# ScalarE's order in the first step of an attention unit: exponential, denominators' copy, logit copies, exponential

## The chip, the core and the metric

The kernel runs on one core of a Trainium2 chip. The metric is the device time of one execution in microseconds (us), the median over several runs. A profiled execution, taken apart from those, gives the span from its first to its last instruction and a record of every instruction.

Five engines work side by side, each through its own instruction stream: TensorE (PE in the profile, with its weight loads as PEld), VectorE (DVE), ScalarE (ACT), GpSimd (POOL) and SyncE (SP), which here only issues DMA transfers.

## What is computed

The input is 8 images of 512 channels and 32 x 32 positions, all in 32-bit floats. The work is two residual layers, each ahead of a group norm:

```
x = x + L0(groupnorm(x))
x = x + L1(groupnorm(x))

L0:  t = silu(bn(conv1x1(x)))                  512 -> 512, split in two halves of 256
     ys = [t[:256], t[256:]]
     for i in 0, 1:
         z = silu(bn(conv3x3(ys[-1])))         256 -> 256
         q, k, v = conv1x1(z)                  4 heads of 64
         logits = q . (k + r) / 8              1024 x 1024 a head, r = rw + rh
         z = softmax(logits) . v
         ys.append(ys[-1] + silu(bn(conv1x1(z))))
     out = silu(bn(conv1x1(concat(ys))))       1024 -> 512

L1:  a 1x1 convolution whose weights are masked by the arg-max of two tables and permuted
```

The softmax is the part that the change is about. For a query i it needs the maximum of its logits over the 1024 keys, the exponentials of the logits less that maximum, their sum (the denominator), and the product of the exponentials with v, divided by the denominator.

## The kernel before

**Slots and units.** An image has two attention blocks, and a *slot* is one block of one image; there are 16 slots, and the images go through them in pairs. A slot is cut into four *units*: two pairs of heads (`hp`) by two halves of 512 queries (`half`). So there are 64 units. A unit handles two heads at once, one in each half of a tile's second axis, with queries along the free axis and 128 keys at a time on the partitions: eight key tiles, `t` from 0 to 7. The exponentials of a key tile stand in an `st` tile of 128 x 2 x 512.

**What a unit does**, by the methods of class `Unit`:

- `logits(t)` (line 503): two matmuls into two PSUM banks `lg`; ScalarE copies both to `st` (line 518); VectorE keeps the running maximum `mx` (line 523).
- `top()` and `spread()` (lines 525 and 534): transposes on TensorE and a reduction on VectorE (line 532) turn `mx` into the negated maximum of each query, and transposes spread it over the partitions in the PSUM tile `mb`.
- `soften(t)` (line 543): VectorE adds `mb` to `st` in place (line 545).
- `exponent(t)` (line 547): ScalarE takes the exponential of `st` in place (line 549); GpSimd adds it into the sum `acc` in four pieces (line 556), from t = 1 on.
- `values(t)` (line 558): two matmuls of v with `st` accumulate into the PSUM tile `po` over all t (line 563).
- `finish()` (line 572): matmuls of `acc` with ones give the denominators in a PSUM bank `den` (line 577); ScalarE copies them to the tile `rb` (line 580).
- `divide(part)` (line 582): VectorE takes the reciprocal of half of `rb` (line 584) and multiplies `po` with it into `q` (line 586).

**The pipeline over units.** The main loop goes through the units. A unit's logits are made one unit ahead, while the unit before it is in its exponentials. The inner loop (line 1057) has four steps, t = 0, 2, 4 and 6, each for two key tiles. In the first step, t = 0, the unit before (`before`) is brought to its end: its denominators, its last two value products, its division. Beside that the step softens the unit's own tiles 0 and 1, takes their exponentials, and makes logits 0 and 1 of the next unit (`nxt`). In a step t > 0 the order is: soften t and t + 1, exponential of t, value products of t - 2 and t - 1, logits t and t + 1 of the next unit, exponential of t + 1.

**Background work.** Between these steps `advance` emits pieces of other work: the 1x1 and 3x3 convolutions of other images, their batch norms with Silu on ScalarE (`bn_silu`, line 130), group norms (line 165), the projections to q, k and v, and the last layer. The 3x3 convolution is computed from transformed rows: VectorE makes its inputs (lines 280 to 288).

**What sets the order.** The compiler orders each engine's instructions itself, by program order and by when it thinks that they can run, except where the kernel forbids it. Three helpers do so: `pe_turn`, `in_turn` and `act_turn` tie an instruction to the one before that went through the same helper, on TensorE, VectorE and ScalarE. On ScalarE the logit copies and the exponentials are in this chain; the batch norms, the group norms and, before the change, the denominators' copy are not. The two reciprocals and the two products of `divide` are not in VectorE's chain either. Waits between engines are added by the compiler.

**Buffers.** PSUM is cut into three pools: `ps_m` with the one `mb` tile (two banks' worth), `ps_o` with one buffer for `po`, and `ps_f` with five banks that `lg`, `den`, the transposed maxima and all convolutions share. There are ten `st` tiles. The tile `rb` comes from a pool of three that the background's batch norms share.

The core of the order in a step:

```
                u.soften(t)
                u.soften(t + 1)
                if t:
                    u.exponent(t)
                ...
                    lag.values((t - 2) % KT)
                    lag.values((t - 1) % KT)
                ...
                    nxt.logits(t)
                    nxt.logits(t + 1)
                ...
                if not t:
                    u.exponent(t)
                u.exponent(t + 1)
```

Of the kernel before, what the change touches and what calls it, by code (L numbers as in the profile page):

```python
# [39 lines left out]
def conv_preact_kernel(ctx: ExitStack, tc: tile.TileContext, x, cv1, cv2, mcv1, qkv, mcv2, bn, rw, rh, conv, s_in, t_in, out):  # L40
    nc = tc.nc
# [26 lines left out]
    def bank(name):  # L68
        return ps_f.tile([P, HALF], F32, tag="bank", name=name)

    def half_tile(name):
        return tp.tile([P, HALF], F32, tag="t", name=name)
# [115 lines left out]
    def act_turn(instruction):  # L188

        if act_last:  # L190
            tc.add_manual_dep(instruction.ins, act_last.pop().ins.name, IN_ORDER, reason="order of ScalarE")
        act_last.append(instruction)
# [3 lines left out]
    def pe_turn(instruction):  # L196

        if pe_last:
            tc.add_manual_dep(instruction.ins, pe_last.pop().ins.name, IN_ORDER, reason="order of TensorE")
        pe_last.append(instruction)  # L200
# [293 lines left out]
    class Unit:  # L494
# [76 lines left out]

        def finish(self):

            den = bank(f"den_{self.name}")
            for h in range(2):
                pe_turn(
                    nc.tensor.matmul(den[HD * h : HD * h + HD], ones[:, :HD], self.acc[:, h], start=True, stop=True)  # L577
                )
            self.rb = half_tile(f"rb_{self.name}")
            nc.scalar.copy(self.rb, den)  # L580

        def divide(self, part):
            r = ts(part, HALF // 2)
# [325 lines left out]
    def slot_filler(s):  # L909

        prev = slots[s - 1] if s else (None, 0)
        nxt = slots[s + 1] if s + 1 < len(slots) else (None, 0)
        todo, needed = [], 0.0

        def add(us, g):
            nonlocal needed
            todo.append((us, g))
            needed += us

        im, i = nxt  # L920
        add(8.0, bg.take(8.0))
        if im and i == 1:
            add(7.0, im.conv_m2(0))
            add(0.0, call(im.transform, 1, 3.0, 1.0))
            add(9.0, bg.take(9.0))
        products = im.conv3(i) if im else iter(())
        if prev[1] == 1:
            if im:
                add(21.3, (us for _, us in zip(range(16), products)))
            add(7.0, prev[0].conv_m2(1))  # L930
            add(0.0, call(lambda: finishing(prev[0])))
        if im:
            add(10.7 if prev[1] == 1 else 32.0, products)
            add(7.0, bg.take(7.0))
        if im:
            add(21.0, im.project(i))
        if s + 2 < len(slots) and slots[s + 2][1] == 0:
            add(0.0, call(slots[s + 2][0].load_y))
            add(0.0, call(slots[s + 2][0].transform, 0, 8.0, 1.3))
        rest = SHARE - needed if im else 70.0  # L940
        if rest > 0:
            todo.append((rest, bg.take(rest, wait=True)))
        total = sum(c for c, _ in todo)
        return needed, total, todo
# [76 lines left out]
    before = None  # L1021
    for s in range(len(slots)):
        needed, total, todo = slot_filler(s)
        state = {"done": 0.0}

        def filler():
            for us, g in todo:
                start = state["done"]
                for cost in g:
                    clock.tick(cost)  # L1030
                    state["done"] += cost
                    yield

                state["done"] = max(state["done"], start + us)

        fill = filler()

        def advance(share):
            goal = max(share * total, min(1.0, share / 0.74) * needed + 0.1)
            while state["done"] < goal:  # L1040
                if next(fill, "end") == "end":
                    break

        steps = 4 * (KT + 2)
        for j in range(4):
            u = units[4 * s + j]
            nxt = units[4 * s + j + 1] if 4 * s + j + 1 < len(units) else None
            base = j * (KT + 2)

            advance((base + 0.7) / steps)  # L1050
            u.top()
            clock.tick(0.9)
            advance((base + 1.4) / steps)
            u.spread()
            clock.tick(0.9)
            advance((base + 2) / steps)
            for t in range(0, KT, 2):
                if before and t == 0:
                    before.finish()
                    clock.tick(0.9)  # L1060
                u.soften(t)
                u.soften(t + 1)
                if t:
                    u.exponent(t)

                lag = u if t else before
                if lag:
                    lag.values((t - 2) % KT)
                    lag.values((t - 1) % KT)
                    clock.tick(2.0)  # L1070
                if before and t == 0:
                    before.divide(0)
                    before.divide(1)
                if nxt:
                    nxt.logits(t)
                    nxt.logits(t + 1)
                    clock.tick(2.0)

                if not t:
                    u.exponent(t)  # L1080
                u.exponent(t + 1)
                advance((base + 4 + t) / steps)
            before = u
        for _ in fill:
            pass

    before.finish()
    before.values(KT - 2)
    before.values(KT - 1)
    before.divide(0)  # L1090
# [57 lines left out]
```

## Time and profile before

| What | Value |
|---|---|
| Time, median of 3 runs | 3188.08 us (3178.91 to 3189.95) |
| The profiled execution's own time | 3188.51 us |
| Its span | 3186.8 us |
| Mean granted TensorE clock | 0.993 of full speed |
| TensorE busy, 0 to 265 us (start) | 242.57 us |
| TensorE busy, 265 to 3060 us (units) | 2724.63 of 2795 us |
| TensorE busy, 3060 to 3187 us (end) | 118.68 of 127 us |
| ScalarE busy in the units | 1598.76 us |
| VectorE busy in the units | 1890.44 us |
| ScalarE table loads ahead of line 549 | 110, 1283 ns each |
| Reciprocal, line 584 | 128, 1723 ns each |
| Exponential, line 549 | 512, 1068 ns each |
| Logit copy, line 518 | 1024, 596 ns each |

The profile names an instruction by line, engine, operation and tiles (written <- read). A bracket at a timeline line's end gives the engine's idle time just before it and what ended that. The chain is the work that ended last, followed back from the last instruction; a releaser is what ended a wait, and of several it is the last. Durations of matmuls are modelled, so a small overlap of two rows on TensorE is none. Where a unit is named by a time, that is about when its first step stands in the trace.

### The profile page before, as it was taken

To read this page: it belongs to the slowest core of one execution; us is meant where nothing else is said; L and a number is where in the kernel's file an instruction comes from. 1 tells how busy PE (TensorE), PEld (TensorE's weight loads), DVE (VectorE), ACT (ScalarE), POOL (GpSimd) and SP (SyncE) were. 2 spreads that over 40 slices of the span, in tenths; PEclk is the share of its full clock that TensorE was granted. 3 is DMA by queue.
4 is the path that set the end of the run, shared out by engine and by line. 5 is a ranking of instruction groups with operands and counts; after the bars stand their busy time and mean duration, and the time that the engine had idled before them with its cause. 6 is when DMAs were issued, how large, how long until landed. Compare 5 with 4: busy or idle time off the path is not lost.

```text
span 3186.8 us, 34171 instructions
## 1 busy us (share of the span) xinstructions
PE 3085.9 (97%) x11668; PEld 1522.9 (48%) x11668; DVE 2050.6 (64%) x2718; ACT 1717.3 (54%) x2347; POOL 1395.3 (44%) x1867
## 2 busy tenths in 40 slices
PE   7999999999999999999999999999999999999999
PEld 3645444454445454454445454454445454453333
DVE  5446576667666676667666676667766676666742
ACT  3255765854655555544656455554656455555631
POOL 2114444446444454445444454355434454455420
PEclk9999999999999999999999999999999999999999
DMA  8851442421233232424233332424233332413366
GB/s 294 287 187 63 154 161 83 149 79 65 88 109 129 93 119 70 148 86 137 89 109 129 119 114 75 139 83 142 90 113 132 110 122 71 145 63 129 110 212 216
DMA packets 142014, 399.35 MB, mean 125 GB/s; under 512 B 13072, under 2 KB 14352, under 8 KB 141840
## 3 DMA queue, kind: packets, MB, share of 16 engines
q1 hardware_dynamic: 141120, 396.94, 36.4%
q8 instruction: 92, 1.51, 0.2%
q14 instruction: 82, 0.67, 0.1%
q10 hardware_dynamic: 720, 0.23, 0.0%
HBM read 317.42 MB, written 79.69 MB: 125 GB/s over the span
## 4 chain that ended last, share of the span: by engine, by line
PE 70%; DVE 7%; ACT 5%; issue 3%; DMA 2%; POOL 1%; ACTq 0%; DVEq 0%; SPq 0%; POOLq 0%
PE m L313 14%; PE cv L175 12%; PE lg L511 11%; PE po L563 11%; PE qk L175 6%; PE l L175 6%; PE v L405 3%; PE m L175 2%; DVE st L545 2%; PE mb L540 2%; ACT st L518 2%; PE mt L531 2%; PE den L577 2%; DVE mx L523 1%; ACT st L549 1%
## 5 line engine op out<-in xcount | busy, mean ns | idle before, releaser
L556 POOL TENSOR_TENSOR sum<-sum,st 128x256 f32<-128x256 f32 x1536 | 1126.1, 767 | 570.1 <-ACT st L549 565.0
L523 DVE TENSOR_TENSOR mx<-mx,lg 128x512 f32<-128x512 f32 x768 | 477.8, 681 | 412.2 <-ACT st L518 412.2
L549 ACT ACTIVATE st<-st 128x1024 f32<-128x1024 f32 x512 | 539.1, 1068 | 340.2 <-DVE st L545 338.8
L518 ACT COPY st<-lg 128x512 f32<-128x512 f32 x1024 | 524.4, 596 | 351.7 <-PE lg L511 306.6
L545 DVE TENSOR_TENSOR st<-st,mb 128x1024 f32<-128x1024 f32 x512 | 603.7, 1213 | 63.6 <-PE mb L540 63.6
L313 PE MATMUL m<-plane,w_m 128*128 128x256 f32 x2304 | 537.4, 388 | 21.8 <-DVE x2r L487 9.0
L556 POOL TENSOR_TENSOR sum<-st,st 128x256 f32<-128x256 f32 x256 | 188.0, 766 | 789.4 <-ACT st L549 789.3
L563 PE MATMUL po<-st,v 128*64 128x512 f32 x2048 | 500.3, 608 | 21.7 <-ACT st L549 14.7
L511 PE MATMUL lg<-q,k 64*128 64x512 f32 x2048 | 513.7, 619 | 1.6 <-ACT y L130 1.5
L313 PEld LDWEIGHTS m<-plane,w_m 128*128 128x128 f32 x2304 | 433.0, 192 | 149.0 <-issue 44.1
L175 PE MATMUL cv<-y,w_cv 128*128 128x512 f32 x1024 | 465.4, 599 | 10.8 <-DVE mx L523 6.2
L511 PEld LDWEIGHTS lg<-q,k 64*128 64x128 f32 x2048 | 178.6, 187 | 330.1 <-issue 266.4
L175 PEld LDWEIGHTS cv<-y,w_cv 128*128 128x128 f32 x1024 | 185.7, 190 | 251.7 <-issue 227.8
L563 PEld LDWEIGHTS po<-st,v 128*64 128x64 f32 x2048 | 128.9, 137 | 327.5 <-issue 228.9
L175 PE MATMUL l<-x,w_l 128*128 128x512 f32 x512 | 235.8, 603 | 10.3 <-DVE mx L523 10.0
L175 PE MATMUL cv<-x,w_cv 128*128 128x512 f32 x512 | 233.4, 603 | 8.5 <-ACT x L165 2.4
L175 PE MATMUL qk<-z,w_qkv 128*128 128x512 f32 x512 | 234.0, 600 | 1.7 <-DVE mx L523 1.7
L584 DVE RECIPROCAL rb<-rb 128x256 f32<-128x256 f32 x128 | 215.4, 1723 | 30.6 <-ACT rb L580 30.5
L532 DVE TENSOR_REDUCE nm<-mt 128x4 f32<-128x512 f32 x128 | 82.4, 685 | 158.6 <-PE mt L531 158.5
L580 ACT COPY rb<-den 128x512 f32<-128x512 f32 x64 | 37.3, 583 | 226.9 <-PE den L577 226.9
L175 PEld LDWEIGHTS l<-x,w_l 128*128 128x128 f32 x512 | 92.7, 190 | 132.3 <-issue 107.2
L175 PEld LDWEIGHTS cv<-x,w_cv 128*128 128x128 f32 x512 | 94.3, 192 | 126.4 <-issue 107.3
(145 smaller groups left out, 2404.3 us busy)
## 6 DMA issues: line engine op xcount, KB each, us to landing
w_m<-w_m SPq DMA_DIRECT2D x96, 768.0 KB, 4.8
w_cv<-in_cv SPq DMA_DIRECT2D x90, 512.0 KB, 3.5
y<-y SPq DMA_DIRECT2D x64, 512.0 KB, 4.4
x<-in_x SPq DMA_DIRECT2D x56, 512.0 KB, 5.4
y<-y SPq DMA_DIRECT2D x64, 256.0 KB, 3.5
k<-r SPq DMA_DIRECT2D x32, 512.0 KB, 3.6
res<-y SPq DMA_DIRECT2D x32, 512.0 KB, 4.0
xr<-in_x SPq DMA_DIRECT2D x32, 512.0 KB, 4.0
```

The lines of the kernel that those rows point to most:

```text
L175: nc.tensor.matmul(ps, w, moving, start=(n == 0), stop=(n == len(terms) - 1))
L313: nc.tensor.matmul(ps[:, ts(co, 256)].rearrange("p (t x) -> p t x", x=F), w[:, co, c, dx], u[:, 9 * c : 9 * c + 8, dx : dx + F], start=(j ...
L405: nc.tensor.matmul(ps[:, ts(j, P)], z[:, c, ts(4 * j4 + j, P)], w[:, c, 512 + P * hp : 512 + P * hp + P], start=(c == 0), stop=(c == IT - 1),)
L511: nc.tensor.matmul(lg[h], self.k[r, ts(t, P)], self.q[r, self.hp, ts(self.half, HALF)], start=True, stop=True)
L518: act_turn(nc.scalar.copy(st[:, h], lg[h]))
L523: in_turn(nc.vector.tensor_tensor(self.mx[:, h], so_far[:, h], lg[h], ALU.max))
L532: nc.vector.tensor_reduce(self.nm[:, h], mt, AX.X, ALU.max, negate=True)
L545: in_turn(nc.vector.tensor_tensor(st, st, flat(self.mb), ALU.add))
L549: act_turn(nc.scalar.activation(st, st, AF.Exp))
L556: nc.gpsimd.tensor_tensor(flat(self.acc)[:, part], flat(so_far)[:, part], st[:, part], ALU.add)
L563: nc.tensor.matmul(self.po[HD * h : HD * h + HD], self.v[:, t, ts(h, HD)], self.st[t][:, h], start=(t == 0), stop=(t == KT - 1),)
L584: nc.vector.reciprocal(self.rb[:, r], self.rb[:, r])
```

## The change

The change splits `finish()`: the matmuls of the denominators stay in it, and the copy to `rb` goes to a new method `copy_den()`, where it also goes through `act_turn`. In a unit's first step the exponential of tile 0 is no longer taken after the next unit's logits but right behind the softens, and `copy_den()` of the unit before follows it. So ScalarE's chain in this step, which was four logit copies, exponential 0, exponential 1, with the denominators' copy outside it, is now exponential 0, denominators' copy, four logit copies, exponential 1. Behind the last unit `copy_den()` follows `finish()` as it did inside it. In the first unit, which has no unit before it, only the exponential moves.

```diff
         def finish(self):
 
-            den = bank(f"den_{self.name}")
+            den = self.den = bank(f"den_{self.name}")
             for h in range(2):
                 pe_turn(
                     nc.tensor.matmul(den[HD * h : HD * h + HD], ones[:, :HD], self.acc[:, h], start=True, stop=True)
                 )
+
+        def copy_den(self):
             self.rb = half_tile(f"rb_{self.name}")
-            nc.scalar.copy(self.rb, den)
+            act_turn(nc.scalar.copy(self.rb, self.den))
...
                 u.soften(t)
                 u.soften(t + 1)
-                if t:
-                    u.exponent(t)
+                u.exponent(t)
+                if before and t == 0:
+                    before.copy_den()
 
                 lag = u if t else before
...
                     nxt.logits(t + 1)
                     clock.tick(2.0)
 
-                if not t:
-                    u.exponent(t)
                 u.exponent(t + 1)
                 advance((base + 4 + t) / steps)
...
     before.finish()
+    before.copy_den()
     before.values(KT - 2)
```

## The prediction

> **What bounds the kernel now.** I read the page's busy shares and chain first, then what TensorE waits for, then the timeline of single units.
>
> ```profile
> PE 3085.9 (97%) x11668; PEld 1522.9 (48%) x11668; DVE 2050.6 (64%) x2718; ACT 1717.3 (54%) x2347; POOL 1395.3 (44%) x1867
> ...
> PE 70%; DVE 7%; ACT 5%; issue 3%; DMA 2%; POOL 1%; ACTq 0%; DVEq 0%; SPq 0%; POOLq 0%
> ...
> L549 ACT ACTIVATE st<-st 128x1024 f32<-128x1024 f32 x512 | 539.1, 1068 | 340.2 <-DVE st L545 338.8
> ...
> L580 ACT COPY rb<-den 128x512 f32<-128x512 f32 x64 | 37.3, 583 | 226.9 <-PE den L577 226.9
> ```
>
> TensorE is busy 97% of the span and carries 70% of the chain; ScalarE is busy 54%. The 226.9 us that ScalarE sits idle in front of the denominators' copy are therefore no loss in themselves. The edit can only return what TensorE loses to a late exponential. The view of waits, for TensorE (total us, times, longest), gives that:
>
> ```profile
> PE po L563 <- ACT st L549: 14.7, 12, 3.7
> ...
> PE po L563 <- DVE mx L523: 6.9, 8, 2.3
> ```
>
> Both rows are the value product; of their 21.6 us about 17 lie in the first matmul of values(0), one such wait in some 17 units. Two units show how it comes about. The first is a unit at 2155 us with no table load (start, us, engine, line, out<-in, count, idle before and its releaser):
>
> ```profile
> 2155.40 2.35 DVE L545 TENSOR_TENSOR st<-st,mb 128x1024 f32<-128x1024 f32 x2 [0.95 <-PE mb L540]
> ...
> 2156.37 0.58 ACT L580 COPY rb<-den 128x512 f32<-128x512 f32 x1 [4.79 <-PE den L577]
> 2157.67 3.36 DVE L584 RECIPROCAL rb<-rb 128x256 f32<-128x256 f32 x2
> ...
> 2159.16 2.05 ACT L518 COPY st<-lg 128x512 f32<-128x512 f32 x4 [2.20 <-PE lg L511]
> ...
> 2160.94 0.69 DVE L586 TENSOR_TENSOR q<-po,rb 128x256 f32<-128x256 f32 x2
> ...
> 2161.07 2.04 ACT L549 ACTIVATE st<-st 128x1024 f32<-128x1024 f32 x2
> ...
> 2162.21 2.02 PE L563 MATMUL po<-st,v 128*64 128x512 f32 x8 [1.23 <-ACT st L549]
> ```
>
> The first soften ends near 2156.6, but its exponential runs at 2161.07, behind the denominators' copy and four logit copies. TensorE waits 1.23 us for it. The second is at 1654 us, where a Silu ran before:
>
> ```profile
> 1654.24 0.78 ACT L130 ACTIVATE cv2s<-cv,bn_b,bn_s 128x512 f32<-128x512 f32 x1 [7.84 <-PE cv L175]
> ...
> 1655.29 0.58 ACT L580 COPY rb<-den 128x512 f32<-128x512 f32 x1 [0.27 <-PE den L577]
> ...
> 1656.39 3.35 DVE L584 RECIPROCAL rb<-rb 128x256 f32<-128x256 f32 x2
> ...
> 1658.08 2.05 ACT L518 COPY st<-lg 128x512 f32<-128x512 f32 x4 [2.20 <-PE lg L511]
> ...
> 1660.15 1.28 ACT L549 ACT_TABLE_LOAD   x1
> 1661.44 2.95 ACT L549 ACTIVATE st<-st 128x1024 f32<-128x1024 f32 x3
> ...
> 1662.55 2.02 PE L563 MATMUL po<-st,v 128*64 128x512 f32 x8 [0.48 <-ACT st L549]
> ```
>
> Here the Exp table is loaded after the copies as well, so 1.28 us more stand in front of both exponentials, while ScalarE had idled 2.20 us before the copies. Counting units by the timeline, 36 of 63 have such a load at this place.
>
> **What the Trainium skill says.** "ScalarE: Activation LUTs", What ACT_TABLE_LOAD costs: about 1283 ns for the load of any set; the trace agrees (1283 ns mean). "TensorE: Matmul & The Clock Gate", Architectural detail: ScalarE and VectorE are strict first-in-first-out; the trace agrees, the exponential above does not pass the copies although its operand is ready. "PSUM — Partial Sum Buffer", Specifications: 8 banks; the kernel's pools take 2 + 1 + 5 of them, so `po` has one. "TensorE: Matmul & The Clock Gate", Part 1: an idle window of about 3.4 us halves the clock; in the unit at 2911, after an idle of 3.72 us, eight value matmuls take 3.68 us against 2.02 above, which agrees.
>
> **The change part by part.** Nothing is added or removed: the same copy, 128 exponentials of 1.07 us and 256 copies in these steps. No DMA moves. What moves is ScalarE's order, and with the chain the denominators' copy gets a fixed place behind exponent(0).
>
> *Exponent(0) ahead.* It starts when its soften ends. At 2155: 2156.67 to 2157.74. The table load goes in front of it: at 1654 after the Silu, 1655.02 to 1656.30, then the exponential to 1657.37. It is hidden by the idle time that stood before the copies. The copies wait for logits at 2159.16 and 1658.08; exponential plus copy end at 2158.34 and 1657.97, so the copies, and the maxima and banks behind them, stay where they are. Working this out for each unit from its own rows, only the first three or four and those with a group norm on ScalarE differ, by about 1 us each way: 0, within -2 and +3.
>
> *Exponent(1)* starts right behind the copies: earlier by one exponential (about 0.9) in units without the load, by 2.3 in the 36 with it. At 1654 it ends 1661.2 instead of 1663.4. The sums of GpSimd begin earlier by the same; GpSimd is 44% busy, so that is slack.
>
> *The denominators' copy behind exponent(0).* At 2155 it moves from 2156.37 to 2157.76, ending at 2158.34; the reciprocal moves from 2157.67 to 2158.40, +0.73. At 1654 it moves to 1657.39, the reciprocal to 1658.03, +1.64. Reciprocals and the two products take 3.96 us, and after them alone the single `po` bank is free for values(0). At 2155 the products end at 2162.36 and values(0) starts at 2162.41, 0.20 later than now, with values(1) 0.12 later since its exponential is ready by then: the removed wait is replaced by the wait for the bank. So 10 units like this pay 0.1 each, +1.1. The unit at 722, whose wait is longest among them, gains 0.4. At 1654 values(0) is held to 1662.05 by the bank and to 1662.24 by TensorE, values(1) goes from 1663.50 to 1663.11: -0.4, three units, -1.2. The unit at 1066 (four norms among the copies) -1.4, that at 2910 (idle 3.72) -2.1, one at 2990 -0.2, the last unit about +1. Sum of this place: 1.1 - 0.4 - 1.2 - 1.4 - 2.1 - 0.2 + 1 = -3.2, say -3.
>
> *VectorE later by 0.73 to 1.64.* Mostly hidden: VectorE has idle of 0.4 to 4 us within 8 to 12 us behind the reciprocals. Three units (883, 1603, 2324) have none for 20 us, since the input transform stands there, and TensorE waits 1.46 for VectorE at their end: 3 x 0.73 = +2.2.
>
> *What the earlier exponent(1) triggers.* In the units at 1293, 2012 and 2730 a chain runs from the copies over load, exponentials, three Silus (2740.14), a residual add, a load of `res` (issued at 2743.27, 6.2 us), and the input transform on VectorE to three waits of TensorE: 0.60, 1.55 and 3.54 us in the last, 17 us in all three units. This chain starts up to 2.3 earlier, bounded by the m2 outputs (TensorE 2739.3). I take -2 a unit, -6, between 0 (the load comes late for another reason) and -12 (waits gone and the clock kept).
>
> Sum: -3 + 2.2 - 6 = -7 us, against the profiled execution's 3188.51 us (span 3186.8): 3181.5. Its own time is within 0.5 of the median 3188.08, so I give 3181.
>
> **The rivals.** *All waits on a late exponential go* (faster): about 17 us at values(0), plus up to 12 from the chain above, less 3 paid elsewhere: -22 to -26, 3164. For it: the compiler orders the unchained instructions, reciprocals among them, anew and may find better places. Against it: the single `po` bank, which holds at 2155 without any guess.
>
> *A late soften blocks the queue* (slower): exponent(0) now stands ahead of five copies, so a soften that is late by x makes the copy of denominators late by x, then reciprocal, `po` bank and TensorE. Now the softens end 1 to 2.5 us before the copies are due; it decides from about 0.8 us later, as when a residual add or statistics are put ahead of them on VectorE (0.69 each), or when a Silu lands between the two exponentials and costs two table loads, 2.57. At 0.7 in half of the units that is +22: 3210. For it: the order of these is unchained. Against it: in 60 units of this trace the margin holds.
>
> *It moves nothing*: waits traded one for one, -2 to +8, 3191; for it is the short unit above, where the edit does just that.
>
> **How the numbers follow.** Forecast 0.47, nothing moved 0.16, all waits gone 0.25, queue blocked 0.12. A measurement of this kernel tells about 0.5% (16 us) from no change: faster is below 3172, slower above 3204. Forecast and nothing moved lie within: 0.61 with a small part of their tails; faster 0.26, slower 0.13. Forecast alone: 3172 to 3189. For 8 in 10 it reaches from 3163 (first rival) to 3203, leaving out most of the second.
>
> **What would show it.** The order on ScalarE in each unit: load, exponential, copy, four copies, exponential. The wait of ScalarE before the denominators' copy (226.9 us) mostly turns into a wait for soften. Reciprocals 0.7 to 1.6 us after their place now; at the units at 2155 a value product still waiting about 1.4 us, now for VectorE's product; the waits on L549 in values(0) down from 14.7 to some 5. About 110 Exp loads as before. I am wrong if the loads grow by 20 or more, if the softens end later against the den matmuls, or if waits at the chain of the unit at 2730 stay 5 us.

## The result, and the profile after

The changed kernel takes 3196.93 us (median of 10 runs, 3194.66 to 3206.62), the kernel before 3187.60 us beside it (10 runs, 3178.91 to 3189.96): 1.0037 times as long, interval 1.0026 to 1.0048. It is slower by 0.37%; 3181 was forecast, with a range from 3172 to 3189. The profiled execution took 3196.4 us, with a span of 3194.7, 7.9 more than before.

The page after: busy times, shares of the chain, and the group of the exponentials.

```profile
PE 3094.2 (97%) x11668; PEld 1527.5 (48%) x11668; DVE 2049.5 (64%) x2718; ACT 1757.3 (55%) x2373; POOL 1393.9 (44%) x1867
...
PE 76%; DVE 7%; ACT 5%; issue 3%; DMA 3%; POOL 0%; ACTq 0%; SPq 0%; DVEq 0%; POOLq 0%
...
L549 ACT ACTIVATE st<-st 128x1024 f32<-128x1024 f32 x512 | 548.1, 1072 | 611.5 <-DVE st L545 610.5
```

ScalarE has 26 instructions more (2373 against 2347) and is busy 40 us longer, TensorE 8.3 us longer with the same 11668 matmuls. The groups of ScalarE by shape show what the 26 are (total us, mean ns | idle before and its releaser).

```profile
L130 ACT ACT_TABLE_LOAD x124 | 159.1, 1283 | 9.7 <-PE m L175 7.1 <-issue 0.3
L549 ACT ACT_TABLE_LOAD x123 | 157.8, 1283 | 2.2
...
L582 ACT COPY rb<-den 128x512 f32<-128x512 f32 x64 | 36.9, 576 | 7.3 <-PE den L577 7.1
```

They are table loads: 13 more ahead of exponentials (123 against 110), 13 more ahead of batch norms' Silus (124 against 111). The 26 loads are 33 of the 40 us. The copy of the denominators waits 7.3 us instead of 226.9, as the new order must make it, and the exponentials' wait for soften rises from 338.8 to 610.5. Neither says anything of the loss.

TensorE's waits after (us, times, longest):

```profile
PE po L563 <- DVE q L588: 14.3, 12, 2.4
PE lg L511 <- ACT y L130: 5.3, 3, 3.2
PE po L563 <- ACT st L549: 4.6, 3, 1.8
PE cv L175 <- ACT y L130: 4.0, 2, 2.5
```

The rows before that go with the second and the last of these:

```profile
PE cv L175 <- ACT y L130: 1.9, 1, 1.9
PE lg L511 <- ACT y L130: 1.5, 1, 1.5
```

The wait of value products for a late exponential falls from 14.7 to 4.6, and 14.3 us of waits for VectorE's product, that is for the `po` bank, take its place. All waits of value products together fall only from 21.6 to 18.9. The waits for a Silu `y` grow: those of the logit matmuls from 1.5 to 5.3, those of the convolutions' matmuls (`cv`) from 1.9 to 4.0. The wait of 1.5 stood at 217 us and stands there still, ahead of unit 1. New are 0.5 at 361.72, 2.5 at 383.87 and 3.2 at 417.64, all in units 3 and 4, and they lead to the cause.

**Where the time went.** I cut the run at the matmuls of the denominators, which mark the first step of each unit. The start is 2.0 us longer; the units from the first such matmul to the fifth (units 1 to 4) take 16.7 us more; all later units together take 10.7 less; the end is 0.1 shorter. So in this profile the change does gain over 59 units, and loses more than that in four. The windows view of that stretch, before (window, its length, then busy us of each engine with its instructions, granted clock, DMA share, GB/s):

```profile
core 0: us, PE busy (x) PEld busy (x) DVE busy (x) ACT busy (x) POOL busy (x), PEclk, DMA share, GB/s
260.80:451.70 190.90, 184.07 (x683) 86.68 (x682) 124.40 (x174) 132.63 (x173) 83.94 (x115) 0.99 0.40 135
```

The same stretch after:

```profile
262.80:470.40 207.60, 194.61 (x685) 89.71 (x684) 123.72 (x174) 145.30 (x182) 84.02 (x115) 0.96 0.37 124
```

The work is the same; ScalarE has nine instructions more, all table loads (34 against 25), 11.5 us at 1283 ns. TensorE's idle time, length less busy, goes from 6.8 to 13.0 us. And the clock falls from 0.99 to 0.96: by the clock records of the traces, TensorE ran at half speed for 3.4 us of the stretch before and for 17.1 after, in windows of 3.4 us. Half of that is lost if TensorE is busy throughout, so I estimate 6.9 us more. 6.2 and 6.9 are 13.1 of the 16.7; 3.6 us are not split further.

**How it comes about.** Unit 4's first step shows it. The timeline before (start, us, engine, line; the bracket is the idle time before and its releaser):

```profile
402.93 2.28 PE L511 MATMUL lg<-q,k 64*128 64x512 f32 x8
403.27 0.76 ACT L130 ACTIVATE y<-cv,bn_b,bn_s 128x512 f32<-128x512 f32 x1
403.94 0.57 ACT L580 COPY rb<-den 128x512 f32<-128x512 f32 x1
...
406.33 1.52 ACT L165 ACTIVATE x<-x,go_a,gr_a 128x512 f32<-128x512 f32 x2 [1.83 <-DVE rb L584]
...
407.75 2.02 ACT L518 COPY st<-lg 128x512 f32<-128x512 f32 x4
...
409.79 1.28 ACT L549 ACT_TABLE_LOAD   x1
411.08 2.00 ACT L549 ACTIVATE st<-st 128x1024 f32<-128x1024 f32 x2
```

The same step after:

```profile
409.70 1.08 PE L577 MATMUL den<-sum,ones 128*64 128x512 f32 x4
...
412.43 1.98 PE L511 MATMUL lg<-q,k 64*128 64x512 f32 x6
413.14 1.28 ACT L549 ACT_TABLE_LOAD   x1
414.44 1.06 ACT L549 ACTIVATE st<-st 128x1024 f32<-128x1024 f32 x1
415.51 1.28 ACT L130 ACT_TABLE_LOAD   x1
416.81 0.78 ACT L130 ACTIVATE y<-cv,bn_b,bn_s 128x512 f32<-128x512 f32 x1
417.48 1.51 ACT L165 ACTIVATE x<-x,go_a,gr_a 128x512 f32<-128x512 f32 x2
...
417.64 1.84 PE L511 MATMUL lg<-q,k 64*128 64x512 f32 x2 [3.23 <-ACT y L130]
418.89 0.57 ACT L582 COPY rb<-den 128x512 f32<-128x512 f32 x1
419.36 2.05 ACT L518 COPY st<-lg 128x512 f32<-128x512 f32 x4
...
421.43 1.28 ACT L549 ACT_TABLE_LOAD   x1
422.72 1.06 ACT L549 ACTIVATE st<-st 128x1024 f32<-128x1024 f32 x1
```

Before, the Silu runs first, then both copies; the table is switched once and serves both exponentials. After, the Exp table is loaded for exponential 0, the Silu's for the Silu that follows it, and Exp's again for exponential 1. The Silu reads a convolution's PSUM bank, from the five banks that the logits share. With the Silu late the bank is late, and TensorE waits 3.23 us in the middle of the next unit's logits. The Silu and the two norms (`x`) stand between exponential 0 and the denominators' copy although the program emits that copy right behind the exponential: they are outside ScalarE's chain, and the compiler puts them where it sees fit. "TensorE: Matmul & The Clock Gate", Architectural detail, in the Trainium skill, has ScalarE strictly first-in-first-out, and the trace agrees: the denominators' copy ran at 418.89, behind the Silu and the norms, although its matmuls had ended at 410.78 and exponential 0, which it follows in the chain, at 415.50.

ScalarE's order in the whole stretch, one line from one denominators' copy D to the next, ending in the first steps of units 2, 3, 4 and 5 (c logit copy, E exponential, T table load, y a Silu of `y`, x a group norm, dot for the rest):

```
before  ccccEEEccccEET..ccccTETyTEccccETy...D
        ccccTEE.E.ccccE.E..ccccETyTEccccETyxxyxxyD
        ccccTEETyTEcxccxcxxETyyTEccccETyyccccTETyyyxxyD
        xxccccTEET...TEccccET.yTEcccxcExxTyxTEccccETy.D
after   ccccEEccccEET..ccccTETyTEccccETy..TE.D
        ccccE.E.ccccE.E..ccccETyTEccccETyxxyxxTETyD
        ccccTETyTEcxcxccxxETyTETyccccTETyTEccccETyyyxxTETyxxD
        ccccTET..TET.ccccTET.yxxTEccccETyxxTEccccETy.TED
```

In front of D, before has Silus and no exponential; after has `TETyD` in unit 3 and `TETyxxD` in unit 4. The wait of 2.5 us at 383.87 falls in a later step of unit 3, where two Silus that shared a table load now have an exponential between them (`ETyTETycccc` for `ETyyTEcccc`), and the second is late. `y` is the output of the 1x1 convolution of the other images, which is the background here. It is a matter of the start: all 64 of these Silus run in the first 1100 us, 60 of them in the first 710.

### The profile page after: what moved, and what is told of

The parts are those of the page before. It is cut to its first block, busy times and chain, and to the rows that moved or that the text cites. A ratio compares the mean times of both kernels' runs of the same rounds, so it can differ in the third digit from the quotient of the medians.

```text
span 3194.7 us, 34196 instructions
## 1 busy us (share of the span) xinstructions
PE 3094.2 (97%) x11668; PEld 1527.5 (48%) x11668; DVE 2049.5 (64%) x2718; ACT 1757.3 (55%) x2373; POOL 1393.9 (44%) x1867
## 4 chain that ended last, share of the span: by engine, by line
PE 76%; DVE 7%; ACT 5%; issue 3%; DMA 3%; POOL 0%; ACTq 0%; SPq 0%; DVEq 0%; POOLq 0%
PE m L313 15%; PE cv L175 14%; PE lg L511 12%; PE po L563 11%; PE qk L175 6%; PE l L175 6%; PE v L405 3%; PE m L175 3%; DVE st L545 2%; PE mb L540 2%; PE mt L531 2%; PE den L577 1%; ACT st L549 1%; DVE mx L523 1%; DMA x<-in_x 1%
## 5 line engine op out<-in xcount | busy, mean ns | idle before, releaser
L549 ACT ACTIVATE st<-st 128x1024 f32<-128x1024 f32 x512 | 548.1, 1072 | 611.5 <-DVE st L545 610.5
L563 PE MATMUL po<-st,v 128*64 128x512 f32 x2048 | 499.0, 604 | 18.9 <-DVE q L588 14.3
L130 ACT ACT_TABLE_LOAD x124 | 159.1, 1283 | 9.7 <-PE m L175 7.1
L549 ACT ACT_TABLE_LOAD x123 | 157.8, 1283 | 2.2
```

The costliest lines, as they stand in the source:

```text
L130: nc.scalar.activation(dst, src, AF.Silu, bias=bn_b[:, col : col + 1], scale=bn_s[:, col : col + 1])
L549: act_turn(nc.scalar.activation(st, st, AF.Exp))
L563: nc.tensor.matmul(self.po[HD * h : HD * h + HD], self.v[:, t, ts(h, HD)], self.st[t][:, h], start=(t == 0), stop=(t == KT - 1),)
```

## The experiments

Two theories stood at first: A, the loss lies in the first units, where this background's Silus get between exponential 0 and the denominators' copy; or B, the rival, it is paid in every unit, by the copy and division that now stand behind an exponential. Each kernel was timed in rounds beside the kernel before; the medians and ratios below are against those.

### The order by slot

`e1_late_units_only` has the new order from slot 2 on and the old one in slot 1 (units 0 to 3), `e2_first_units_only` the reverse.

```diff
-                u.exponent(t)
-                if before and t == 0:
+                ahead = s > 0
+                if t or ahead:
+                    u.exponent(t)
+                if before and t == 0 and ahead:
                     before.copy_den()
...
+                if not (t or ahead):
+                    u.exponent(t)
                 u.exponent(t + 1)
```

In e2 the condition is `s == 0`. With the old order, the copy stands right behind `finish()`, outside the chain, as before.

> The new order from the fifth unit on; the first four units keep the old one. Theory A (the loss sits in the first four units, where a batch norm's Silu of the start falls between exponential 0 and the denominators' copy; the other units gain): the stretch of the first four units takes about 188 us again, as before the change, the rest keeps its gain of about 9 us, total about 3179. Rival B (the loss is spread: the denominators' copy behind the exponential holds the single po bank everywhere): stays at 3192 to 3196.

> The new order in the first four units alone. Theory A: all of the loss and none of the gain, 3188 + 16 = about 3204, the stretch of the first four units about 204 us. Rival B: 3188 to 3190, since only 4 of 64 units have the new order.

e1 took 3190.87 us against 3185.92, 1.0014 (1.0004 to 1.0024); e2 3197.90, 1.0036 (1.0025 to 1.0048). So slot 1 alone loses about as much as the whole change, yet the later slots alone do not gain. The cuts at the units say why: in e1, units 1 to 4 change by 0, -0.4, +1.1 and +8.8 us. Unit 4's first step still has the image background, but unit 4 belongs to slot 2. I had cut in the wrong place. The units from 5 on are 6.3 us shorter in e1; in e2, with the old order there, they are 7.1 shorter too, so the length of this stretch in one profile is uncertain by as much as the gain. What scatters is the clock: e2 had 13.7 us less at half clock in these units than before, and e1 3.4 more. With half of that taken into account, an estimate, e2 is 0.3 us shorter there and e1 8.0.

### The order from unit 5 on

`e6_from_unit5` moves the cut to `4 * s + j > 4`, `e7_units_1to4` is its complement (`<= 4`), and `e9_change_again` is the changed kernel once more, on the same chip in turn.

> The new order from the first step of unit 5 on. The runs before cut at the wrong place: the unit that loses most (about 9 us) is the fourth, whose first step lies in the second slot, so the run from the fifth unit on still had it. Here ScalarE's order up to that step is the old one. Theory A (loss in the first steps of units 1 to 4, from Silus between exponential 0 and the denominators' copy): 200 to 470 us as before the change, the rest a gain of about 5: 3180 to 3184 against 3186. Rival B (loss spread): 3190 or above.

> The complement: the new order in the first steps of units 1 to 4 alone. Theory A: 3198 to 3204, all of it before 470 us. Rival B: 3186 to 3188.

> The change again, on the same chip as the other three: 3195 to 3198; and whether its trace shows the same stretch of loss (262 to 470 us), so that one profile of each isn't trusted alone.

| Kernel | Time, us | Against before, 3186.66 us | Units 1 to 4, before 190.9 us | Half clock there, us |
|---|---|---|---|---|
| e6, new order from unit 5 on | 3182.81 | 0.9987 (0.9977 to 0.9996) | 193.6 | 6.8 |
| e7, new order in units 0 to 4 | 3209.12 | 1.0070 (1.0058 to 1.0082) | 204.5 | 10.2 |
| e9, the change | 3201.34 | 1.0049 (1.0036 to 1.0062) | 207.2 | 13.7 |

This settles where. Without the first units the change gains 3.9 us, and e6 is faster than both kernels; the first units alone lose 22.5. Together that is +18.6, against the +14.7 of the whole, which agrees within the intervals. The profiled execution of e7 was the fastest of its five, 7.1 us under their median, so its row shows less than those 22.5. The windows view of the stretch in e6:

```profile
262.80:456.40 193.60, 185.52 (x683) 86.99 (x682) 124.38 (x174) 133.89 (x174) 84.03 (x115) 0.98 0.39 133
```

and in e9, the repeat of the change:

```profile
263.10:470.30 207.20, 192.89 (x683) 88.52 (x682) 123.61 (x174) 145.03 (x182) 83.95 (x115) 0.97 0.37 125
```

ScalarE's 182 instructions, nine more than before, come with the loss and are 174 without it. The number of loads in the whole run does not decide: e6 has 238, 16 more than before, and is faster.

### The Silus in the chain

If the place of the Silus is the cause, the change should lose most of its cost once they are fixed in front of the exponential. `e8_silu_chained` is the whole change, with the Silus of the 1x1 convolution put through `act_turn` up to unit 4 (`bn_silu` returns its instruction for this).

```diff
-                    bn_silu(t, ps, BN_CV1 + IT * cp + co)
+                    silu = bn_silu(t, ps, BN_CV1 + IT * cp + co)
+                    if early:
+                        act_turn(silu)
...
+            early[:] = [1] if 4 * s + j <= 4 else []
```

> The change as it is, and up to unit 4 the Silus of the start's convolution go through ScalarE's chain, so that each stands ahead of exponential 0 where it stood between that and the denominators' copy. Theory A in its narrow form (it is the Silu's place): most of the 16 us come back, 3184 to 3188, and the waits of the logit matmuls on that Silu (5.3 us) go. Rival C (the exponential ahead of the copies is itself what hurts there, by its wait for a soften): 3195 or above.

3191.57 us, 1.0014 (1.0006 to 1.0023): 4.9 us above before, where the change stands 14.7 above it in the same rounds. Two thirds of the loss in time went with the place of the Silus. ScalarE's order now has them in front, and `ETyyTE` is back in unit 3. The last line below is unit 4's, up to the copy in unit 5's first step:

```
e8      ccccE.E.ccccE.E..ccccETyTEccccETyxxyxxyTED
        ccccETyTEcxcxccxxETyyTEccccETyTEccccETyyyxxyTED
        xxccccET..TET.ccccTET.yxTEccccExTyxxTEccccETy.TED
```

The stretch of units 1 to 4:

```profile
264.10:464.20 200.10, 189.75 (x683) 89.23 (x682) 123.58 (x174) 136.54 (x176) 84.11 (x115) 0.96 0.38 129
```

Units 1 to 3 are nearly as long as before (+0.2, +1.3, +0.3), the waits for `y` within the units are gone and the table loads are 28. Unit 4 still loses 7.5, with 13.7 us at half clock instead of 3.4 and 3.1 us more of idle time. TensorE waits 1.4 to 2.8 us four times from 411 us on, where before it waits twice, 2.8 and 1.5 us. The first of the four is for the denominators' copy, behind table load and exponential 0:

```profile
411.85 0.49 PE L156 MATMUL gv_a<-gd_a,gmat 128*128 128x4 f32 x2 [1.71 <-ACT rb L585]
```

This wait is the new order's own, but with the next one, for the logit copies, it makes 3.1 us, where before one of 2.8 stood. So what makes unit 4 longer stays open: its group norms, also outside the chain, stand in another order there in later steps, but no run tests them alone.

### The denominators' copy by itself

Two kernels test the rival. `e3_den_first` exchanges the first two links of the chain: the copy, then exponential 0. `e4_den_free` keeps exponential 0 ahead and takes the copy out of the chain, back behind `finish()`.

```diff
-                u.exponent(t)
                 if before and t == 0:
                     before.copy_den()
+                u.exponent(t)
```

```diff
-            act_turn(nc.scalar.copy(self.rb, self.den))
+            nc.scalar.copy(self.rb, self.den)
...
                     before.finish()
+                    before.copy_den()
```

> Denominators' copy ahead of exponential 0 in ScalarE's chain, otherwise the change. Theory A: in the first units the Silu now stands ahead of both, so the loss of 16 us goes too; besides, reciprocals are no longer 0.7 to 1.6 us late, values(0) waits less for the po bank (14.3 us of waits on VectorE's product down to about 7): about 3173 to 3178. Rival B agrees on the po bank and gives 3180 to 3184. If the order of these two doesn't matter, 3197.

> Exponential 0 ahead of the logit copies, the denominators' copy outside the chain as before the change. The order that ScalarE gets keeps the Silu between exponential 0 and the denominators' copy in the first units. Theory A: the loss there stays, 3190 to 3197. Rival B (the copy's place in the chain is the loss): the copy is free again, 3180 or below.

Both are as slow as the change or slower: e3 3197.87 us, 1.0040 (1.0026 to 1.0054), e4 3205.99, 1.0054 (1.0036 to 1.0072). The 3173 to 3178 that I expected of e3 was a miss. TensorE's waits in e3:

```profile
PE po L563 <- ACT st L549: 12.7, 9, 2.6
PE po L563 <- DVE q L588: 11.0, 12, 1.8
```

The copy is earlier, but with load and exponential behind it the logit copies and exponential 1 are no earlier, so the late exponential is back (12.7 us against 4.6) while the bank still costs 11.0. e4 loses 18.5 us in units 1 to 4 and has 260 table loads in all, against 222 before and 248 in the change: free of the chain, the copy gives the compiler one more instruction to place. Both kernels also start 4 to 6 us late before unit 1, which I did not trace.

The units of e3 set a limit to theory A. Unit 4 is as long as before there (-0.3), with its Silus in front of the copy. But unit 3 loses 7.7, though no Silu stands between its copy and its exponential 0. TensorE waits 1.1 to 2.5 us four times in it, at full clock, and ScalarE's order, up to the copy in unit 4's first step, has other free instructions moved, four group norms ahead of logit copies:

```
before  ccccTEETyTEcxccxcxxETyyTEccccEETyccccTETyyyxxyD
e3      TEccccEETyxxxxccccTETyTETyccccTEETyccccTETyyyxxyD
```

So taking the copy from behind the exponential does not bring the time back, and the Silus' place in the first step is one way among others in which the free instructions of these units cost time. That the copy's place costs nothing at all is not shown.

### A second bank for `po`

To see what the wait for the `po` bank hides, `e10_po_two_banks` gives `po` two banks and the shared pool four instead of five, on top of e6; `e11_before_po_two_banks` does the same to the kernel before.

```diff
-    ps_o = pool("ps_o", 1, space=PSUM)
-    ps_f = pool("ps_f", 5, space=PSUM)
+    ps_o = pool("ps_o", 2, space=PSUM)
+    ps_f = pool("ps_f", 4, space=PSUM)
```

> The new order from unit 5 on, and PSUM cut anew: two banks for po, four instead of five for logits, denominators and convolutions. If the single po bank holds back the gain of the earlier exponential: the waits of values(0) on VectorE's product (11.8 us) go to about 0. What the lost shared bank costs is not known from the traces: den and four logit banks are in use at once, so that the last logit matmul waits for the denominators' copy, about 1 us a unit or more. So slower in all, 3200 to 3300; the row of the po waits is what counts.

> Control for the last: the order of before the change with the same PSUM cut. Here po waits are on the exponential, so the row of waits of values(0) on ScalarE stays at 10 to 20 us; time as much above 3187 as the lost bank costs. If the po bank limits the gain, the new order gains more against this control than the 4 us that it gains with one po bank, about 10.

e10 took 3464.42 us, 1.0866 (1.0828 to 1.0905), e11 3468.64, 1.0888 (1.0870 to 1.0906). The bank that was taken away costs some 280 us. TensorE's waits in e10:

```profile
PE lg L511 <- DVE mx L523: 39.7, 56, 1.2
PE po L563 <- ACT st L549: 18.4, 18, 1.8
```

and in e11:

```profile
PE lg L511 <- DVE mx L523: 54.5, 67, 3.0
PE po L563 <- ACT st L549: 29.2, 32, 3.7
```

No value product waits for VectorE's product any more, and the new order takes 10.8 us off the late exponential. But the difference in time is 4.2 us, about what e6 gains with one bank, and the two intervals overlap. That the single bank holds back a larger gain is not shown; logits now wait for their own banks, and that decides.

## Why the prediction was wrong

The step that failed is the one that put exponential 0 ahead at nothing: "only the first three or four and those with a group norm on ScalarE differ, by about 1 us each way: 0, within -2 and +3". It measured +16.7, in units 1 to 4 alone. I had seen that these units differ, but worked their rows out with the background left in its old place. Moving one link of the chain also moved the unchained Silus and norms around it: from the front of the exponential to behind it. The mechanism itself stood in the text as a rival: "when a Silu lands between the two exponentials and costs two table loads, 2.57". I had priced it as a thing of half of all units, at a chance of 0.12; it is a thing of the first four, where it costs more than two loads, since behind the Silu wait a PSUM bank, TensorE and its clock. The measured 3196.93 us lie above the range of the forecast, and inside the wider one, up to 3203, that leaned towards this rival. With the Silus chained (e8) two thirds of the loss in time are gone; the last third, 4.9 us, is not explained.

The other steps:

- *The bank takes the place of the exponential.* Right. In the unit that stood at 2155 us, now at 2165, against the start of its den matmul, the reciprocal moved by +0.54 (forecast 0.73), values(0) by +0.12 (forecast 0.20), and the timeline after shows the wait for VectorE's product, 1.35 us where about 1.4 was forecast:

```profile
2167.23 1.06 ACT L549 ACTIVATE st<-st 128x1024 f32<-128x1024 f32 x1 [5.07 <-DVE st L545]
...
2168.19 0.57 ACT L582 COPY rb<-den 128x512 f32<-128x512 f32 x1
...
2168.79 3.37 DVE L586 RECIPROCAL rb<-rb 128x256 f32<-128x256 f32 x2 [0.47 <-ACT rb L582]
...
2171.65 1.09 ACT L549 ACTIVATE st<-st 128x1024 f32<-128x1024 f32 x1
2172.07 0.69 DVE L588 TENSOR_TENSOR q<-po,rb 128x256 f32<-128x256 f32 x2
...
2172.91 1.94 PE L563 MATMUL po<-st,v 128*64 128x512 f32 x8 [1.35 <-DVE q L588]
```

  Exponential 1 starts right behind the copies, ahead of the two products, and is not waited for. The unit as a whole is 0.78 us longer, though (0.77 in e9), where 0.1 was forecast: later in it two matmuls wait 0.37 and 0.11 us more for VectorE's maxima.
- *The gains by unit.* The unit at 2910 gained 2.5 (forecast 2.1), of which some 1.7 is a window of half clock that is gone; the three like that at 1654 gained 0.6 each (0.4), the one at 1066 gained 0.7 (1.4).
- *VectorE later, three units at +0.73.* Not seen in these three: they are 0.6 shorter each, and the waits in them fell from 1.46 to 0.84. The cost came elsewhere, as in the unit at 2155.
- *What the earlier exponential 1 triggers, -6.* A part came: in the units at 1293, 2012 and 2730 the waits fell from 17.2 to 15.1 in all, and the three are 3.6 us shorter together (2.2 in e9). The 0.60 waits went; the longest, for the transform, is 3.5 us in each (before 1.9, 3.5 and 3.5), so the residual's load or the transform behind it is late for a reason other than the exponential.
- *The sum without the first units.* Forecast -7 for the whole; e6 is 3.9 faster, with 2.0 at its start and 2.8 in units 1 to 4 against it, so the later units gain some 9. Their single profiles give -6.3 (e1) to -11.4 (e9), with the old order -3.2 (e7) and -7.1 (e2). With half of the difference in half clock taken off, the five profiles with the new order in all of these units give -7.2 to -10.4, the two with the old one -0.3 and -1.5. So I estimate their gain at 6 to 10. The forecast of the sum holds for them, in part by luck, since its parts are off both ways.
- *The table loads.* "I am wrong if the loads grow by 20 or more": they grew by 26, so this sign came true. But only 9 of these stand in units 1 to 4, and e6 is faster with 16 more than before: the count alone does not decide.

## What to carry to other kernels

When only some of an engine's instructions are in a fixed order, moving one of these moves the free ones around it. List the engine's whole stream by stage, table loads included, and do it for the start by itself, where other background runs than in the steady state: here 59 units could not pay for what four lost. An order that pays in one stage can be asked for in that stage alone, which gave the only version faster than both kernels.

## What was not expected of the hardware

Waits of two to three microseconds can cost TensorE more than their length. "TensorE: Matmul & The Clock Gate", Part 1, speaks of an idle window of about 3.4 us. Here a shorter one was enough, 2.53 us: the clock records have a window of half clock of 3.4 us from 383.8 us on. The timeline after, two groups of twelve matmuls of the same shape, the first without a wait, the second behind one:

```profile
363.02 5.40 PE L175 MATMUL cv<-x,w_cv 128*128 128x512 f32 x12
...
383.87 7.05 PE L175 MATMUL cv<-x,w_cv 128*128 128x512 f32 x12 [2.53 <-ACT y L130]
```

The twelve matmuls take 1.65 us longer, which is about half of a window of 3.4 us. At a wait of 2.57 us at 345.93 another such window begins. Not every wait of this length has one: in e9, the same program, the wait at this place is 2.52 us and the clock stays full, so that the stretch had 13.7 us at half clock instead of 17.1. Part of the run-to-run spread of this kernel goes with the clock: of its ten runs in the result, the four with a mean granted clock of 0.992 or 0.993 took 3194.7 to 3197.2 us, the three with 0.989 or 0.990 3199.7 to 3206.6.
